# Retention values made in pass 1: one 256-column matmul for score and value, values kept in DRAM

## The chip, the cores and the metric

The kernel runs on one NeuronCore of a Trainium2 chip. A NeuronCore has a matrix engine (TensorE, PE in the profile), a vector engine (VectorE, DVE), a scalar engine (ScalarE, ACT), GpSimd (POOL) and SyncE (SP), which here only issues DMAs. Each engine works through its own list of instructions in order and waits on semaphores where an instruction needs another engine's result or a DMA. SBUF is the on-chip memory of 128 partitions, PSUM the accumulator memory that TensorE writes, in eight banks of 128 x 512 fp32. The metric is device time in microseconds (us), the median of several executions. All data is fp32.

## The reference, cut to what matters

The layer takes 64 sequences of 128 tokens of width 512. It adds a gated retention over a context, then a gated feed-forward network. `xn` is the layer-normed x; H is 4 heads of HD = 128.

```python
Q, K, V = (einsum('bshd,hde->bshe', heads(t), Wh) for t in (xn, ctx, ctx))
scores = einsum('bshe,bthe->bhst', Q, K) / sqrt(HD)
A = maximum(abs((scores * decay).sum(axis=0)), 1.0)      # summed over all 64 sequences
O = einsum('hst,bthe->bshe', A, V).reshape(b, s, dim)
Y = groupnorm(O) * gn_gamma + gn_beta
x = x + tanh(g_xattn) * ((relu(xn @ wg_w) * Y) @ wo_w)
x = x + tanh(g_ffn) * ffn(layernorm(x))                    # silu(gate) * up, then down
```

The sum over all sequences forces two passes: A needs the scores of every sequence before the first O can be made. Q and K share Wh, so the scores are xn (Wh Wh^T) ctx^T; the product Wh Wh^T is called `gram`.

## The kernel before, in words

The 64 sequences are worked in 16 groups of four (GB = 4, TOK = 512 tokens).

**Pass 1** loops over the groups. Iteration g runs three generators beside each other: `prepare` (L407: layer norm of group g, its transposition by TensorE into `xnT`), `scores` of group g-1 (L428) and `project` of group g-1 (L452: relu(xn wg) by seven products of a Strassen-like scheme, stored in DRAM as `w_scr` through ScalarE's DMA queue). `scores` makes, for each head, pq = gram x xnT over 512 columns (L432), copies it to SBUF by ScalarE (`q`, L436), and then adds for each of the 4 sequences and 4 heads a matmul of 128 columns into one PSUM bank (`acc`, L442), which gathers over all groups. The stationary operand of that matmul is the context tile c_t[j][:, h, :]. In the same iterations the weights of pass 2 are prepared (`prepare_weights`, L379): raw blocks are loaded by SP, summed by GpSimd and stored into `gu_scr`, `dn_scr` and `wo_scr`; two buffers hold raw blocks, so a block's load waits for an earlier block's store. SP's list also holds the loads of x (five tiles of two sequences, `load_x`, L103) and of context (five tiles of one sequence, `load_ctx`, L117).

Between the passes `acc` is multiplied by the decay, and its absolute value is clamped at 1 (L511 to L514): that is `attn`.

**Pass 2** runs the FFN of group g (`ffn`, L732) beside `attended` of group g+1 (L608: the wo products, the residual and the second layer norm) and `retention` of group g+2 (L527). `retention` loads the context a second time, makes the values V = ctx Wh by 16 matmuls of 128 columns (L534; stationary: the same c_t[j][:, h, :]), copies them to `v` by ScalarE (L538), multiplies by attn (`po`, L544), normalises and, through a DRAM round trip that transposes (`moved`, L187, with tiles of tag `sq` or `v`), scales w.

**The order of the work.** The generators are woven together by `interleave` (L30) in proportion to step counts written by hand. That gives a program order. The Tile framework then makes one list for each engine: it takes the instruction that is earliest in program order among those that its own estimate says are ready, so an instruction may move ahead of earlier ones, and loads go out as soon as a buffer of their tag is planned free. Buffers are given by tag: tiles of one tag share a fixed number of buffers (`bufs`), in program order. After the build the lists are fixed. `tc.issue_after` keeps weight traffic behind the last x load on SP.

PSUM holds three rotating banks under tag `mm` (ps_mm, L98) and five fixed ones (bank_a, bank_f, bank_b, bank_c0, bank_c1); `acc` is bank_c1 during pass 1.

Of the kernel before, what the change touches and what calls it, by code (L numbers as in the profile page):

```python
# [10 lines left out]
F32 = mybir.dt.float32  # L11
# [30 lines left out]
def after(steps, gen):  # L42

    for _ in range(steps):
        yield
    yield from gen
# [3 lines left out]
def flamingo_gated_layer(  # L50
# [36 lines left out]
    SQ = nc.vector.STREAM_SQUARE_SIZE  # L87
    NQ = P // SQ
# [2 lines left out]
    const = ctx.enter_context(tc.tile_pool(name="const", bufs=1))  # L91
    dram = ctx.enter_context(tc.tile_pool(name="dram", bufs=1, space=DRAM))
    xin = ctx.enter_context(tc.tile_pool(name="xin", bufs=5))
    cin = ctx.enter_context(tc.tile_pool(name="cin", bufs=5))
    att = ctx.enter_context(tc.tile_pool(name="att", bufs=1))
    wide = ctx.enter_context(tc.tile_pool(name="wide", bufs=2))
    stat = ctx.enter_context(tc.tile_pool(name="stat", bufs=4))
# [16 lines left out]
            pair.append(t)  # L114
        return pair

    def load_ctx(b):  # L117
        t = cin.tile([P, H, S], F32, tag="c", name="c_t")
        nc.sync.dma_start(out=t, in_=ctxT[b])
        return t  # L120

    x_next = [load_x(0, 1)]

# [4 lines left out]
    mean_var = const.tile([P, B, 2], F32, name="mean_var")  # L128
    rstd = const.tile([P, B], F32, name="rstd")
    attn = const.tile([P, H, S], F32, name="attn")  # L130
    wh_sb = const.tile([P, H, P], F32, name="wh_sb")
    gamma_sb = const.tile([P, NC], F32, name="gamma_sb")
    beta_sb = const.tile([P, NC], F32, name="beta_sb")
    gs_sb = const.tile([P, NI], F32, name="gs_sb")
# [10 lines left out]
        for n in range(2)  # L145
    ]
    w_scr = dram.tile([NG, 2, P, 2, TOK], F32, name="w_scr")

# [4 lines left out]
    bank_b = ps_bank.tile([P, TOK], F32, name="bank_b")  # L153
    bank_c0 = ps_bank.tile([P, TOK], F32, name="bank_c0")
    bank_c1 = ps_bank.tile([P, TOK], F32, name="bank_c1")
    for seeded in (bank_b, bank_c0):
        for i in range(TOK // P):
            nc.tensor.matmul(
                seeded[:, i * P : (i + 1) * P], lhsT=ident, rhs=ident,
                start=(i == 0), stop=True, skip_group_check=True,  # L160
            )
# [89 lines left out]


    pass1 = ExitStack()
    rows = pass1.enter_context(tc.tile_pool(name="rows", bufs=6))
    once = pass1.enter_context(tc.tile_pool(name="once", bufs=1))

    whT_sb = once.tile([P, H, P], F32, name="whT_sb")
# [7 lines left out]
                in_=wg[k * HN : (k + 1) * HN, e0 : e0 + P].rearrange("(k p) i -> p k i", p=P),  # L265
            )
    x_next.append(load_x(1))
    c_next = [load_ctx(b) for b in range(GB)]
# [4 lines left out]
    nc.scalar.activation(tanh_g, gates, AF.Tanh)  # L273


    gram = once.tile([P, H, P], F32, name="gram")
    pg = ps_mm.tile([P, H, P], F32, tag="mm", name="pg")
    for h in range(H):
        nc.tensor.matmul(
# [15 lines left out]
    def constants():  # L295

        nc.sync.dma_start(out=ds, in_=down_s.partition_broadcast(P))
        nc.sync.dma_start(out=decay, in_=decayT)
        nc.sync.dma_start(out=wh_sb, in_=wh.rearrange("h d e -> d h e"))
        nc.sync.dma_start(out=gamma_sb, in_=gamma.rearrange("(c p) -> p c", p=P))  # L300
        nc.sync.dma_start(out=beta_sb, in_=beta.rearrange("(c p) -> p c", p=P))
        nc.sync.dma_start(out=gs_sb, in_=gate_s)
        nc.sync.dma_start(out=us_sb, in_=up_s)

        cols = slice(REST * P, INTER)
        for m, mat, k in ((GA11, gateT, 0), (GA12, gateT, 1), (7, upT, 0), (GA22, upT, 1)):
            nc.sync.dma_start(
                out=gu_rest[:, m],
                in_=mat[k * HN : (k + 1) * HN, cols].rearrange("(c p) i -> p c i", p=P),
            )  # L310
# [91 lines left out]
            gu_rest[:, GA11], gu_rest[:, GA12], gu_rest[:, 7], gu_rest[:, GA22],  # L402
        )

    acc = bank_c1.rearrange("p (h s) -> p h s", h=H)

    def prepare(g, x_t, xnT):  # L407

        n = GB if g else 1
# [16 lines left out]
            yield  # L426

    def scores(g, c_t, xnT):  # L428
        qs = []
        for h in range(H):  # L430
            pq = ps_mm.tile([P, TOK], F32, tag="mm", name="pq")
            nc.tensor.matmul(  # L432
                pq, lhsT=gram[:, h, :], rhs=xnT[:, h, :], start=True, stop=True
            )
            q = rows.tile([P, TOK], F32, tag="row", name="q")
            nc.scalar.copy(q, pq)  # L436
            qs.append(q)
            if h % 2:
                yield
        for j in range(GB):  # L440
            for h in range(H):
                nc.tensor.matmul(  # L442
                    acc[:, h, :],
                    lhsT=c_t[j][:, h, :],
                    rhs=qs[h][:, j * S : (j + 1) * S],
                    start=(g == 0 and j == 0 and h == 0),
                    stop=(g == NG - 1 and j == GB - 1),
                    skip_group_check=True,
                )
            yield  # L450

    def project(g, xnT):  # L452

        b11, b12, b21, b22 = as_b(xnT)
        t = once.tile([P, 4, KC, HT], F32, tag="t1", name="t1")
        combine_b(nc.vector, [t[:, i] for i in range(4)], b11, b12, b21, b22)
        w = once.tile([P, 2, 2, TOK], F32, tag="w1", name="w1")
        m5 = once.tile([P, TOK], F32, tag="m5p", name="m5p")
# [24 lines left out]
        yield  # L483

    pending = None
    weights = prepare_weights()
    for g in range(NG):
        x_t, c_t = x_next.pop(0), c_next
        xnT = wide.tile([P, NC, TOK], F32, tag="xT", name="xnT")
        prep = prepare(g, x_t, xnT)  # L490
        next(prep)
        if g == 1:
            gate_weights()
            constants()
        elif g > 1:
            with tc.issue_after(last_load[0].ins):
                next(weights, None)
        interleave(
            (prep, GB),
            (scores(*pending) if pending else None, 2 + GB),  # L500
            (project(pending[0], pending[2]) if pending else None, 7),
        )
        x_next.append(load_x((g + 2) % NG))
        c_next = [load_ctx((g + 1) % NG * GB + j) for j in range(GB)]
        pending = (g, c_t, xnT)
    for _ in weights:
        pass
    interleave((scores(*pending), 1))


    nc.vector.tensor_mul(attn, acc, decay)  # L511
    absd = rows.tile([P, H, S], F32, tag="row", name="absd")
    nc.scalar.activation(absd, attn, AF.Abs)
    nc.vector.tensor_scalar_max(attn, absd, 1.0)  # L514

# [8 lines left out]
            ws.append(w)  # L524
        return ws

    def retention(g, c_t, ws):  # L527

        helper = nc.vector if g < 3 else nc.gpsimd
        v = att.tile([P, H, GB, P], F32, tag="v", name="v")  # L530
        for j in range(GB):
            pv = ps_mm.tile([P, H, P], F32, tag="mm", name="pv")
            for h in range(H):
                nc.tensor.matmul(  # L534
                    pv[:, h, :], lhsT=c_t[j][:, h, :], rhs=wh_sb[:, h, :],
                    start=True, stop=True,
                )
            nc.scalar.copy(v[:, :, j, :], pv)  # L538
            yield

        o = att.tile([P, GB, H, P], F32, tag="yT", name="o")
        for h in range(H):
# [7 lines left out]
                nc.scalar.copy(o[:, :, h, :], po)  # L550
            yield
        if g:
            sq = att.tile([P, NQ, NC, GB, SQ], F32, tag="v", name="sq")
        ons = []
        for j in range(GB):
            oj = o[:, j].rearrange("p h e -> p (h e)")
# [51 lines left out]
    def attended(g, x_t, ws, x1nT):  # L608
# [53 lines left out]
        yield  # L662

        if g:
            sq = att.tile([P, NQ, NC, GB, SQ], F32, tag="v", name="sq")
        for j in range(GB):
            xb = x_t[j // 2][:, j % 2, :]
            mv = stat.tile([P, 2], F32, tag="mv", name="mv")
# [14 lines left out]
            moved(x1nT, sq, sq_scr[1][g % 2])  # L683

    WAIT = 5
    RET_STEPS = 8 + WAIT + 2
    ATT_STEPS = 8 + GB

    def new_x1nT():
        return wide.tile([P, NQ, NC, GB, SQ], F32, tag="xT", name="x1nT")  # L690

    x_t, c_t = x_next.pop(0), c_next
    c_next = [load_ctx(GB + j) for j in range(GB)]
    ws = load_gate(0)
    interleave(
        (retention(0, c_t, ws), 12), (after(6, project(pending[0], pending[2])), 16),
    )
    x1nT = new_x1nT()
    pass1.close()
# [216 lines left out]

    def next_retention(g):

        nonlocal c_next, ws
        c_t = c_next  # L920
        ws = load_gate(g)
        yield from retention(g, c_t, ws)
        if g + 1 < NG:
            c_next = [load_ctx((g + 1) * GB + j) for j in range(GB)]

    def late_attended(g, x_t, x1nT):
        yield from attended(g, x_t, ws, x1nT)


    second = next_retention(1)  # L930
    interleave((attended(0, x_t, ws, x1nT), ATT_STEPS), (islice(second, 7), 10))
    pending = (0, x_t, x1nT, combine_tokens(nc.vector, x1nT))
    for g in range(NG - 1):
        x_t = x_next.pop(0)
# [4 lines left out]
        n_steps = ATT_STEPS + RET_STEPS  # L939
        if g == 0:  # L940
            steps.append(late_attended(1, x_t, x1nT))
            n_steps += RET_STEPS - 7
        if g + 2 < NG:
            steps.append(next_retention(g + 2))
        interleave(
# [62 lines left out]
```

## Time and profile before

| | |
|---|---|
| median of 3 runs | 2289.34 us (2286.19 to 2290.49) |
| the profiled execution | 2293.72 us |
| its span on the core | 2291.9 us |
| granted TensorE clock, mean | 0.999 of full |
| DMA traffic | 459.17 MB, mean 200 GB/s |
| HBM read / written | 376.72 MB / 80.61 MB |

The span is the time from the first to the last profiled instruction of the program. Busy time of an engine is the time in which it had an instruction at work; matmuls are pipelined, so the duration of one is longer than the distance to the next. Each fp32 matmul shows as two MATMUL records with a weight load (LDWEIGHTS, PEld) each. In lists of waits, "A <- B" says that A was released by B. SPq, ACTq are the issuing of DMAs.

### The profile page before, as it was taken

What the parts mean: (1) busy time and instruction counts of PE and PEld (TensorE: products, weight loads), DVE (VectorE), ACT (ScalarE), POOL (GpSimd) and SP (SyncE); (2) the same over time, 40 slices, a digit from 0 to 9 for tenths busy, and PEclk for the clock granted to TensorE, in tenths of its full rate; (3) what the DMA queues carried; (4) which work ended last, traced back from release to release, by engine and by line L of the source; (5) the groups of instructions that cost most, each with busy time, mean ns of one, the idle gap of its engine ahead of it and who ended that gap; (6) DMA issues with size and microseconds to landing.
All of it is one profiled execution on the core that took longest, in us unless ns stands there. A gap on an engine that the chain in (4) does not pass through costs nothing. (4 is left out here: it accounts for less than half of the span.)

```text
span 2291.9 us, 28061 instructions
## 1 busy us (share of the span) xinstructions
PE 2263.7 (99%) x10808; PEld 1945.1 (85%) x10808; DVE 861.6 (38%) x1771; ACT 574.7 (25%) x1052; POOL 674.5 (29%) x811
## 2 busy tenths in 40 slices
PE   8999999999999999999999999999999999999999
PEld 7777787888888888888888888888888888888888
DVE  6444534544333333323333423343433333333222
ACT  2333333312222221213131212121222122222221
POOL 4232202322232323232424232423223242323210
PEclk9999999999999999999999999999999999999999
DMA  8777746566565656665666656565657475645541
GB/s 266 264 232 244 248 161 228 189 195 225 178 226 173 219 187 212 197 220 193 218 197 197 208 191 225 181 214 181 214 171 236 158 236 174 230 155 186 167 149 65
DMA packets 158213, 459.17 MB, mean 200 GB/s; under 512 B 16768, under 2 KB 36864, under 8 KB 143360
## 3 DMA queue, kind: packets, MB, share of 16 engines
q1 hardware_dynamic: 152656, 440.34, 58.9%
q10 hardware_dynamic: 5424, 17.04, 1.8%
q8 instruction: 85, 1.39, 0.3%
q14 instruction: 48, 0.39, 0.1%
HBM read 376.72 MB, written 80.61 MB: 200 GB/s over the span
## 5 line engine op out<-in xcount | busy, mean ns | idle before, releaser
L207 PE MATMUL bank_c<-tcomb,gu 128*128 128x256 f32 x1920 | 456.9, 379 | 1.0 <-ACT bank_b L766 0.7
L207 PEld LDWEIGHTS bank_c<-tcomb,gu 128*128 128x128 f32 x1920 | 361.3, 190 | 49.4 <-ACT bank_b L766 1.5
L207 PE MATMUL bank_a<-x1nT,gu 128*128 128x256 f32 x1280 | 302.8, 379 | 1.1 <-ACT x1nT L677 0.7
L207 PEld LDWEIGHTS bank_a<-x1nT,gu 128*128 128x128 f32 x1280 | 242.1, 190 | 34.5 <-ACT x1nT L677 1.2
L247 POOL TENSOR_TENSOR hs<-h,h 128x256 f32<-128x256 f32 x80 | 58.0, 726 | 582.7 <-DVE h L746 582.7
L167 POOL TENSOR_TENSOR rs<-ve,mhalf 128x1 f32<-128x1 f32 x128 | 72.6, 576 | 486.4 <-DVE ve L166 471.2
L745 ACT ACTIVATE sil<-c,gs_sb 128x256 f32<-128x256 f32 x160 | 81.2, 508 | 322.7 <-DVE c L775 183.2
L603 POOL TENSOR_TENSOR w_t<-w_t,yT 128x256 f32<-128x256 f32 x112 | 77.9, 726 | 264.2 <-ACT yT L594 264.2
L207 PE MATMUL bank_b<-x1nT,gu 128*128 128x256 f32 x640 | 151.7, 379 | 0.0
L207 PE MATMUL bank_f<-tcomb,gu 128*128 128x256 f32 x640 | 151.2, 379 | 0.0
L798 PE MATMUL bank_c<-dn_w,hs 128*128 128x256 f32 x640 | 145.0, 382 | 0.0
L775 DVE TENSOR_TENSOR c<-bank_c,m 128x512 f32<-128x512 f32 x80 | 55.0, 688 | 237.6 <-PE bank_c L207 234.2
L798 PE MATMUL bank_f<-dn_w,h 128*128 128x256 f32 x640 | 143.4, 379 | 0.0
L798 PEld LDWEIGHTS bank_f<-dn_w,h 128*128 128x128 f32 x640 | 121.5, 190 | 22.4 <-issue 6.7
L207 PEld LDWEIGHTS bank_b<-x1nT,gu 128*128 128x128 f32 x640 | 121.6, 190 | 22.1 <-issue 6.2
L798 PEld LDWEIGHTS bank_c<-dn_w,hs 128*128 128x128 f32 x640 | 120.3, 190 | 19.7 <-ACT bank_b L875 4.0
L207 PEld LDWEIGHTS bank_f<-tcomb,gu 128*128 128x128 f32 x640 | 121.6, 190 | 16.6
L746 DVE SCALAR_TENSOR_TENSOR h<-bank_a,us_sb,sil 128x256 f32<-128x256 f32 x80 | 38.6, 482 | 240.2 <-ACT sil L745 240.2
L171 DVE BATCH_NORM_STATS2 st<-x_t 128x6 f32<-128x512 f32 x128 | 83.0, 684 | 103.3 <-DMA x_t<-in_x_dram 102.2
L758 ACT COPY bank_c<-bank_a 128x512 f32<-128x512 f32 x80 | 45.6, 570 | 258.6 <-PE bank_a L207 256.8
L746 DVE SCALAR_TENSOR_TENSOR h<-c,us_sb,sil 128x256 f32<-128x256 f32 x160 | 78.3, 489 | 75.1 <-ACT sil L745 75.1
L207 PE MATMUL bank_c<-t,wgc 128*128 128x256 f32 x384 | 92.5, 383 | 0.0
(166 smaller groups left out, 3518.1 us busy)
## 6 DMA issues: line engine op xcount, KB each, us to landing
gu<-gu_scr SPq DMA_DIRECT2D x80, 1024.0 KB, 4.9
dn_w<-dn_scr SPq DMA_DIRECT2D x112, 640.0 KB, 5.1
gu<-gu_scr SPq DMA_DIRECT2D x80, 768.0 KB, 5.9
c_t<-in_ctxT_dram SPq DMA_DIRECT2D x128, 256.0 KB, 4.3
x_t<-in_x_dram SPq DMA_DIRECT2D x62, 512.0 KB, 4.6
sq_scr<-sq SPq DMA_DIRECT2D x30, 1024.0 KB, 4.8
wo_w<-wo_scr SPq DMA_DIRECT2D x112, 256.0 KB, 3.9
w_scr<-w ACTq DMA_DIRECT2D x32, 512.0 KB, 5.8
```

Source lines behind the costliest of these rows:

```text
L167: nc.gpsimd.tensor_tensor(dst, ve, mhalf[:, :n], ALU.pow)
L171: nc.vector.bn_stats(st, src)
L207: nc.tensor.matmul(out, lhsT=w[:, s, k, :], rhs=x_k, start=(start and s == 0 and k == 0), stop=(s == 1 and k == KC - 1), skip_group_check= ...
L247: engine.tensor_tensor(s[0], a21, a22, ALU.add)
L603: (helper if d else nc.gpsimd).tensor_tensor(w, w, yT[:, :, d * KC + k, q * 2 : q * 2 + 2, :], ALU.mult)
L745: nc.scalar.activation(sil, src[:, 0:n], AF.Silu, scale=gs_sb[:, i : i + 1])
L746: nc.vector.scalar_tensor_tensor(dst, src[:, n : 2 * n], us_sb[:, i : i + 1], sil, ALU.mult, ALU.mult)
L758: nc.scalar.copy(bank_c, bank_a)
L775: nc.vector.tensor_add(c22, bank_c, m5)
L798: nc.tensor.matmul(bank[:, i * HN : (i + 1) * HN], lhsT=lhs[:, j, i * P : (i + 1) * P], rhs=dn[:, j, :], start=(start and i == 0 and j == ...
```

## The change

Values move from pass 2 to pass 1. `scores` no longer multiplies the context tile by q alone, but by two blocks of 128 columns at once: q of the sequence and Wh (both lie in one tile `qw`, whose last block holds Wh). The result, 256 columns, is the score part and the value part. Two sequences share one PSUM bank of tag `mm`: their score parts add up in its first block, their values stand in the second and third. One ScalarE copy takes the three blocks (128 x 384) to SBUF (`both`). The values are stored from there to a new DRAM tensor `v_scr`, two stores per group on SP's queue; the score parts are added by VectorE from SBUF into `attn`. The loop over heads is now outside that over sequences. `both` takes the tags `v`, `sq`, `ys` and `yT`, two of them per group in turn.

In pass 2 `retention` makes no values: `load_values` reads them with one load per group. The context isn't loaded a second time. The context pool has eight buffers instead of five and ends with pass 1. `sq` has a tag of its own, and `gram`, `m5p` and `absd` use tags of other tiles. Step counts of the weaving follow.

```diff
-    def load_ctx(b):
-        t = cin.tile([P, H, S], F32, tag="c", name="c_t")
-        nc.sync.dma_start(out=t, in_=ctxT[b])
-        return t
+    def load_ctx(g):
+        tiles = []
+        for j in range(GB):
+            t = cin.tile([P, H, S], F32, tag="c", name="c_t")
+            nc.sync.dma_start(out=t, in_=ctxT[g * GB + j])
+            tiles.append(t)
+        return tiles
...
-    for seeded in (bank_b, bank_c0):
+    for seeded in (bank_b, bank_c0, bank_c1):
...
-    rows = pass1.enter_context(tc.tile_pool(name="rows", bufs=6))
+    cin = pass1.enter_context(tc.tile_pool(name="cin", bufs=8))
...
+    qw = once.tile([P, H, GB + 1, P], F32, name="qw")
+    nc.sync.dma_start(out=qw[:, :, GB, :], in_=wh.rearrange("h d e -> d h e"))
...
-            q = rows.tile([P, TOK], F32, tag="row", name="q")
-            nc.scalar.copy(q, pq)
-            qs.append(q)
+            nc.scalar.copy(qw[:, h, 0:GB, :], pq)
             if h % 2:
                 yield
-        for j in range(GB):
-            for h in range(H):
-                nc.tensor.matmul(
-                    acc[:, h, :],
-                    lhsT=c_t[j][:, h, :],
-                    rhs=qs[h][:, j * S : (j + 1) * S],
-                    start=(g == 0 and j == 0 and h == 0),
-                    stop=(g == NG - 1 and j == GB - 1),
-                    skip_group_check=True,
-                )
+        for h in range(H):
+            if h % 2 == 0:
+                tags = ("v", "sq") if g % 2 else ("ys", "yT")
+                both = att.tile([P, 2, 2, 3, P], F32, tag=tags[h // 2], name="both")
+            for q in range(2):
+
+                sv = ps_mm.tile([P, 4, P], F32, tag="mm", name="sv")
+                for i in range(2):
+                    j = 2 * q + i
+                    nc.tensor.matmul(
+                        sv[:, 0 : 2 + i : 1 + i, :],
+                        lhsT=c_t[j][:, h, :],
+                        rhs=qw[:, h, j : GB + 1 : GB - j, :],
+                        start=(i == 0),
+                        stop=(i == 1),
+                        skip_group_check=True,
+                    )
+                nc.scalar.copy(both[:, h % 2, q], sv[:, 0:3, :])
+            if h % 2:
+                nc.sync.dma_start(out=v_scr[g, :, h - 1 : h + 1], in_=both[:, :, :, 1:3, :])
+                total = attn[:, h - 1 : h + 1, :]
+                for q in range(2):
+                    if g == 0 and q == 0:
+                        nc.vector.tensor_copy(total, both[:, :, 0, 0, :])
+                    else:
+                        nc.vector.tensor_add(total, total, both[:, :, q, 0, :])
             yield
...
-            (scores(*pending) if pending else None, 2 + GB),
+            (scores(*pending) if pending else None, 2 + H),
...
-        c_next = [load_ctx((g + 1) % NG * GB + j) for j in range(GB)]
+        if g + 1 < NG:
+            c_next = load_ctx(g + 1)
...
-    nc.vector.tensor_mul(attn, acc, decay)
-    absd = rows.tile([P, H, S], F32, tag="row", name="absd")
+    nc.vector.tensor_mul(attn, attn, decay)
+    absd = att.tile([P, H, S], F32, tag="m1", name="absd")
...
-    def retention(g, c_t, ws):
+    def load_values(g):
+        v = att.tile([P, H, GB, P], F32, tag="v", name="v")
+        nc.sync.dma_start(out=v, in_=v_scr[g].rearrange("p h q i e -> p h (q i) e"))
+        return v
+
+    def retention(g, v, ws):
 
         helper = nc.vector if g < 3 else nc.gpsimd
-        v = att.tile([P, H, GB, P], F32, tag="v", name="v")
-        for j in range(GB):
-            pv = ps_mm.tile([P, H, P], F32, tag="mm", name="pv")
-            for h in range(H):
-                nc.tensor.matmul(
-                    pv[:, h, :], lhsT=c_t[j][:, h, :], rhs=wh_sb[:, h, :],
-                    start=True, stop=True,
-                )
-            nc.scalar.copy(v[:, :, j, :], pv)
-            yield
...
-            sq = att.tile([P, NQ, NC, GB, SQ], F32, tag="v", name="sq")
+            sq = att.tile([P, NQ, NC, GB, SQ], F32, tag="sq", name="sq")
...
-    RET_STEPS = 8 + WAIT + 2
+    RET_STEPS = 4 + WAIT + 2
...
-        c_t = c_next
+        v = load_values(g)
         ws = load_gate(g)
-        yield from retention(g, c_t, ws)
-        if g + 1 < NG:
-            c_next = [load_ctx((g + 1) * GB + j) for j in range(GB)]
+        yield from retention(g, v, ws)
```

More of the change, by code (lines that the diff above doesn't have):

```diff
@@ L93, in flamingo_gated_layer @@
     xin = ctx.enter_context(tc.tile_pool(name="xin", bufs=5))
-    cin = ctx.enter_context(tc.tile_pool(name="cin", bufs=5))
     att = ctx.enter_context(tc.tile_pool(name="att", bufs=1))
@@ L130, in flamingo_gated_layer @@
     attn = const.tile([P, H, S], F32, name="attn")
-    wh_sb = const.tile([P, H, P], F32, name="wh_sb")
     gamma_sb = const.tile([P, NC], F32, name="gamma_sb")
@@ L147, in flamingo_gated_layer @@
     w_scr = dram.tile([NG, 2, P, 2, TOK], F32, name="w_scr")
+    v_scr = dram.tile([NG, P, H, 2, 2, P], F32, name="v_scr")
     bank_a = ps_bank.tile([P, TOK], F32, name="bank_a")
@@ L267, in flamingo_gated_layer @@
     x_next.append(load_x(1))
-    c_next = [load_ctx(b) for b in range(GB)]
+    c_next = load_ctx(0)
+    qw = once.tile([P, H, GB + 1, P], F32, name="qw")
+    nc.sync.dma_start(out=qw[:, :, GB, :], in_=wh.rearrange("h d e -> d h e"))
     gates = const.tile([P, 2], F32, name="gates")
@@ L273, in flamingo_gated_layer @@
     nc.scalar.activation(tanh_g, gates, AF.Tanh)
-    gram = once.tile([P, H, P], F32, name="gram")
+    gram = att.tile([P, H, P], F32, tag="wo", name="gram", bufs=3)
     pg = ps_mm.tile([P, H, P], F32, tag="mm", name="pg")
@@ L298, in constants @@
         nc.sync.dma_start(out=decay, in_=decayT)
-        nc.sync.dma_start(out=wh_sb, in_=wh.rearrange("h d e -> d h e"))
         nc.sync.dma_start(out=gamma_sb, in_=gamma.rearrange("(c p) -> p c", p=P))
@@ L403, in rest_weights @@
         )
-    acc = bank_c1.rearrange("p (h s) -> p h s", h=H)
     def prepare(g, x_t, xnT):
@@ L428, in scores @@
     def scores(g, c_t, xnT):
-        qs = []
         for h in range(H):
-            pq = ps_mm.tile([P, TOK], F32, tag="mm", name="pq")
+            pq = ps_mm.tile([P, GB, S], F32, tag="mm", name="pq")
             nc.tensor.matmul(
@@ L457, in project @@
         w = once.tile([P, 2, 2, TOK], F32, tag="w1", name="w1")
-        m5 = once.tile([P, TOK], F32, tag="m5p", name="m5p")
+        m5 = att.tile([P, TOK], F32, tag="m1", name="m5p")
         bank_c = bank_c0
@@ L664, in attended @@
         if g:
-            sq = att.tile([P, NQ, NC, GB, SQ], F32, tag="v", name="sq")
+            sq = att.tile([P, NQ, NC, GB, SQ], F32, tag="sq", name="sq")
         for j in range(GB):
@@ L690, in new_x1nT @@
         return wide.tile([P, NQ, NC, GB, SQ], F32, tag="xT", name="x1nT")
-    x_t, c_t = x_next.pop(0), c_next
-    c_next = [load_ctx(GB + j) for j in range(GB)]
+    x_t = x_next.pop(0)
+    v = load_values(0)
     ws = load_gate(0)
     interleave(
-        (retention(0, c_t, ws), 12), (after(6, project(pending[0], pending[2])), 16),
+        (after(3, retention(0, v, ws)), 11), (project(pending[0], pending[2]), 9),
     )
@@ L917, in next_retention @@
     def next_retention(g):
-        nonlocal c_next, ws
-        c_t = c_next
+        nonlocal ws
+        v = load_values(g)
         ws = load_gate(g)
-        yield from retention(g, c_t, ws)
-        if g + 1 < NG:
-            c_next = [load_ctx((g + 1) * GB + j) for j in range(GB)]
+        yield from retention(g, v, ws)
     def late_attended(g, x_t, x1nT):
@@ L930, in flamingo_gated_layer @@
     second = next_retention(1)
-    interleave((attended(0, x_t, ws, x1nT), ATT_STEPS), (islice(second, 7), 10))
+    interleave((attended(0, x_t, ws, x1nT), ATT_STEPS), (islice(second, 4), 8))
     pending = (0, x_t, x1nT, combine_tokens(nc.vector, x1nT))
@@ L941, in flamingo_gated_layer @@
             steps.append(late_attended(1, x_t, x1nT))
-            n_steps += RET_STEPS - 7
+            n_steps += RET_STEPS - 4
         if g + 2 < NG:
```

## The prediction

> **What bounds the kernel now.** First the busy table, then the same by stage (columns: stretch, its length, busy time of PE, PE weight load, DVE, ACT, POOL, each with its count; clock; DMA share; GB/s).
>
> ```profile
> PE 2263.7 (99%) x10808; PEld 1945.1 (85%) x10808; DVE 861.6 (38%) x1771; ACT 574.7 (25%) x1052; POOL 674.5 (29%) x811
> ...
> 20.00:340.00 320.00, 310.58 (x1660) 256.45 (x1659) 148.70 (x306) 107.25 (x178) 80.36 (x74) 1.00 0.70 234
> 340.00:396.00 56.00, 51.98 (x268) 40.67 (x267) 27.18 (x51) 20.66 (x36) 11.03 (x11) 1.00 0.59 212
> 396.00:2292.00 1896.00, 1889.33 (x8834) 1638.66 (x8832) 674.13 (x1387) 443.04 (x834) 574.41 (x711) 1.00 0.59 194
> ```
>
> TensorE is the bound in all stages, at full clock. Its idle time is 9.4 us in pass 1 (20 to 340), 4.0 in the passage to pass 2 (340 to 396), 6.7 in the long rest and 8 before 20 us. So a matmul saved is time saved, and a new wait of PE is time lost. The timeline shows what a matmul costs and where pass 1 waits (columns: start, duration, engine, line, tiles, count, and in brackets the idle time before it).
>
> ```profile
> 113.89 1.92 SPq L367 DMA_DIRECT2D gu_raw<-in_gateT_dram  x4
> ...
> 118.44 0.41 SPq L110 DMA_DIRECT2D x_t<-in_x_dram  x1
> 118.95 2.91 SPq L119 DMA_DIRECT2D c_t<-in_ctxT_dram  x3
> ...
> 120.45 1.06 PE L442 MATMUL bank_c<-q,c_t 128*128 128x128 f32 x8
> 121.34 1.89 PE L207 MATMUL bank_c<-t,wgc 128*128 128x256 f32 x8
> ...
> 123.07 1.89 PE L207 MATMUL bank_a<-xnT,wgc 128*128 128x256 f32 x8
> ...
> 124.50 1.29 DVE L171 BATCH_NORM_STATS2 st<-x_t 128x6 f32<-128x512 f32 x2 [6.14 <-DMA x_t<-in_x_dram]
> ...
> 126.49 0.68 DVE L423 COPY xnT<-pt 128x512 f32<-128x512 f32 x1
> ...
> 127.32 1.96 PE L432 MATMUL pq<-xnT,gram 128*128 128x512 f32 x4 [2.36 <-DVE xnT L423]
> ```
>
> Each fp32 matmul is two records (x512 at L442 for 256 matmuls). The durations overlap (pipelined); the cost is from start to start: eight records of 128 columns take 121.34 - 120.45 = 0.89 us, 0.111 each (0.112 over all L442 and L534 records); eight of 256 take 1.73, 0.216 each. The wait: SP loads the next raw weights only when the last sums have been stored; the x load stands behind them on SP; VectorE sits at the statistics of that x, and behind them is the xnT copy that PE needs. The waits (total, times, longest) of 20 to 350 us:
>
> ```profile
> PE pq L432 <- DVE xnT L423: 9.4, 5, 3.5
> SPq L119 <- PE bank_c L442: 115.2, 43, 11.2
> SPq L367 <- DMA gu_scr<-gu_raw: 40.4, 5, 10.6
> ```
>
> Five gate/up weight blocks, five stores waited for, five PE stalls, 1.9 us each. The stores are slow because the stretch after an iteration's start is full of traffic, while its end is not:
>
> ```profile
> 94.00:103.00 9.00, 9.00 (x57) 8.17 (x56) 4.33 (x10) 1.78 (x3) 4.97 (x6) 1.00 0.53 170
> 103.00:114.00 11.00, 11.00 (x52) 8.32 (x51) 5.65 (x12) 5.17 (x9) 1.23 (x1) 1.00 0.83 310
> ```
>
> **The change, part by part.**
>
> 1. PE passes. Removed: 256 score and 256 value matmuls of 128 columns, 1024 records x 0.112 = 114.7 us. Added: 256 of 256 columns, 512 records x 0.216 = 110.6. Net **-4.1 us**. Strided moving operands of 256 columns (x1nT at L207) already run at 0.216, so the two-block operand is taken at that; from below, -4.1 is all there is. A rule speaks against more: the Trainium skill, "TensorE: Matmul & The Clock Gate", section "Wait — 56ns, not 53.3ns?", says that a warm matmul costs its columns plus about 2.5 ns; by it, halving the count saves 512 x 2.5 = 1.3 us. The row's 8 ns per pair is used; the two differ by 2.8 us of 2292. The weight loads of 190 ns were never the bound: they ran at the 0.111 beat.
>
> 2. Where PE's work lies. A group of pass 1 gains 16 x 2 x (0.216 - 0.112) = 3.33 us of PE; a group of pass 2 loses 3.6.
>
> 3. ScalarE. Removed: 64 value copies of 581 ns, 37.2 us. Added: 128 copies of 128x384. Copies of 128x256 take 357 ns and of 128x512 570, so about 463, 59 us in pass 1, on an engine busy 107 of 320 us. Hidden by PE: two copies (0.93 us) per 1.73 us of matmuls, and the three PSUM buffers of `mm` let PE run two tiles ahead. If that cover fails (a copy queued behind the L477 relu, which waits for VectorE 77.0 us in 15 times) PE waits for a buffer; I put this at 0, and at up to 1.2 us in each of 15 iterations, 18 us, at the far end.
>
> 4. VectorE sums: four per group of 128x256 from SBUF, at 419 ns (row L603): 27 us, engine busy 149 of 320. No PE instruction waits for them before the end of pass 1; the prep work queued behind them on VectorE waits with them. Cost 0; covered by PE's 24 us per iteration.
>
> 5. DMA. Pass 1 gains 32 stores of 512 KB (16.8 MB) on SP; each waits for ScalarE copies, and behind it on SP stand raw weights, x and context loads. Gone from SP are most of the 115.2 us of waits for a context buffer: with eight there is room for a whole next group. But the heads are now the outer loop, so the four context tiles come free together, at the end of the scores, and four loads go out in a bunch at the iteration's end. Ahead of the late x load I therefore count both v stores and the three c_t loads that used to follow it (118.95 above): 2 x 0.524 + 3 x 0.262 = 1.83 MB. At the 310 GB/s of the full stretch that is 5.9 us. About 2.6 us of idle stretch (170 of 310 GB/s) before the boundary takes 1.2 us of it: x is 4.7 us later. PE has 3.33 us more to do before it runs dry, so each of the five stalls goes from 1.9 to 1.9 + 4.7 - 3.33 = 3.3 us: **+6.9 us**. Bounds: 0 lateness removes the stalls (-9.4), 5.9 gives +12.9. The skill's "DMA: Bandwidth & Descriptors", section "Specifications", puts the HBM limit of a core at about 358 GB/s; by it the lateness is 5.1 - 1.2 = 3.9, and the sum would be 4 us lower (2291). The row decides, as these are stores and loads mixed in this very stretch.
>
> 6. The passage. Its filler shrinks: the value matmuls of groups 0 and 1 (64 records each) were 7.1 us of PE work beside a chain of latencies (scores, attn, po, o statistics, transposes, w, wo products). Part 1 counts all of it as saved. v of group 0 must now be stored, landed and loaded: the last group's own sums use tag v, so its store (512 KB rows of pass 1: about 5 us) and then 1 MB (gu, 4.9 us) come first: with its first head pair done some 2.5 us before the last score matmul, -2.5 + 5 + 4.9, about 7.5 us after it, against 4.5 for the first po now (350.1 to 354.6). The gate projection of the last group, 12.1 us, covers that, but is then missing where PE already idles before L574 (1.4 us). I take **+3.0** of the 7.1 as not saved, ends 0 and 7.
>
> 7. Pass 2. One 1 MB load per group in place of four of 256 KB; equal bytes. Buffer v has one copy, but since sq has its own tag it is free from the end of one group's po to the next, about 115 us. SP issues loads as soon as a buffer is free (it waits for pv 28 times at L119), so its 4.9 us are hidden by the FFN's matmuls: 0. If the load went out only at its group's own start, 15 x 4.9 = 73 us; w_t, issued up to 320 us ahead in this trace, speaks against it.
>
> 8. wh's earlier load (0.9 us of DMA) and eight more seeding records lie in the start, before the first scores and while PE waits for whT (5.0 us): 0.
>
> Sum: -4.1 + 6.9 + 3.0 = **+5.8 us**. The profiled execution took 2293.7 (span 2291.9 and 1.8 around it), the median shown is 2289.3; the sum is laid on the median: **2295**. On the profile's own scale, a span of about 2298. A measurement can tell about 0.2% (4.6 us) from no change.
>
> **Rivals.**
>
> A. *Stalls vanish* (the other side, faster). One mechanism: the five stalls of L432, 1.9 us each. They are gone as soon as x comes less than 3.33 - 1.9 = 1.4 us later than now: SP no longer sits 115 us on context buffers, and PE has 3.33 us more cover. Then -4.1 - 9.4 + 3.0 = -10.5: 2279. Against it: 1.83 MB at 310 GB/s.
>
> B. *Nothing to see.* x comes about 3.3 us later, as late as the added cover; stalls stay 9.4. -4.1 + 3.0 = -1.1: 2288.
>
> C. *ScalarE becomes the gate of pass 1.* sv tiles need twice the PSUM turns (16 per group for 8), behind ScalarE's in-order waits for L476 and w_scr. With the 1.2 us of part 3: 2295 + 18 = 2313. For it: ACT idled 77.0 us at L477. Against: in the present pass no PE wait on ScalarE is in the list.
>
> **How the numbers follow.** Forecast 0.43 (2290 to 2303 by the bounds of parts 5 and 6), A 0.27, B 0.20, C 0.10. Of the forecast's own range a fifth lies within 0.2%, as does most of B and a little of A: faster 0.29, same 0.24, slower 0.47. Range 2278 to 2310: it takes in A's value and most of the way to C, leaving out one in ten on each side.
>
> **What would show it.** Right: 512 records of 256 columns at sv 0.216 apart; the five pq waits at 2 to 5 us; gu_scr stores landing later than 10.2 us; no L119 waits on scores; pv gone, L544 preceded by no long wait for v in pass 2. Wrong: pq waits gone (A); many PE waits for ScalarE's `both` copies (C); po waiting for v_scr loads group after group (part 7, tens of us); idle in 340 to 396 grown by more than 7.

## The result and the profile after

| | before | after |
|---|---|---|
| median | 2289.2 us (2286.19 to 2293.91) | 2293.05 us (2290.55 to 2294.8) |
| profiled execution, span | 2293.72, 2291.9 us | 2291.79, 2290.0 us |

The ratio of the times is 1.0015, 95% interval 1.0008 to 1.0022: slower by 3.9 us, which is less than the 0.2% that the prediction took as the limit of what can be told. The profiled pair shows the opposite, -1.9 us, because the profiled execution of before lay 4.5 us above its own median and that of after 1.3 below: -1.9 + 4.5 + 1.3 = 3.9. A trace of one execution tells here where time went between stages, but not the sign of the sum.

The page of the changed kernel, its busy table:

```profile
PE 2263.9 (99%) x10304; PEld 1925.2 (84%) x10304; DVE 901.7 (39%) x1835; ACT 601.5 (26%) x1116; POOL 670.9 (29%) x811
```

TensorE has 504 records less (512 by the change, and the eight more of seeding) and the same busy time to 0.2 us: a product that is held up shows partly as a longer one, as will be seen. The same by stage (columns: stretch, length, busy time of PE, PE weight load, DVE, ACT, POOL with counts; clock; DMA share; GB/s). The three stretches are again pass 1, the passage and the rest, but only roughly: the first ends 3.7 us behind the last score matmul here, and 10 us ahead of it in the table of before.

```profile
20.00:396.00 376.00, 375.56 (x1731) 306.21 (x1731) 185.61 (x381) 172.91 (x315) 79.11 (x74) 1.00 0.73 246
396.00:437.00 41.00, 34.44 (x143) 24.05 (x141) 24.81 (x51) 10.75 (x20) 11.68 (x12) 1.00 0.64 237
437.00:2290.00 1853.00, 1842.66 (x8377) 1584.87 (x8376) 680.88 (x1379) 415.21 (x778) 571.79 (x710) 1.00 0.60 199
```

In pass 1 TensorE is idle for 0.4 of 376 us, where it was idle for 9.4 of 320. In the rest it is idle for 10.3 us, where it was 6.7, though there is 50 us less to do. So the changed kernel has won in the one stage and lost in the other. The list of TensorE's waits in pass 1 has one line left:

```profile
PE pt L180 <- DVE xn L201: 0.4, 1, 0.4
```

The five pq stalls are gone in this execution (other traces of the changed kernel show some again, below). In the rest of the run another wait is new (total, times, longest):

```profile
PE bank_c L209 <- DVE c L788: 3.0, 14, 0.2
```

In the kernel before, the same add made TensorE wait once (396 to 2292 us):

```profile
PE bank_c L207 <- DVE c L775: 0.3, 1, 0.3
```

To see where the time went, I cut both traces at the same three events: the first pq matmul, the last score matmul, and the first FFN matmul that reads x1nT. The matmul work moved between the stages is counted in records: 512 sv records of 0.216 us less 512 score records of 0.112 give +53.2 us for pass 1, and the value matmuls of 14 groups, 448 records of 0.112, give -50.2 for pass 2.

| stage | before | after | difference | matmuls alone | gained (-) or lost (+) beyond them |
|---|---|---|---|---|---|
| to the first pq | 17.38 | 19.81 | +2.4 | 0 | +2.4 |
| pass 1, to the last score | 332.61 | 372.45 | +39.8 | +53.2 | -13.4 |
| passage, to the first FFN matmul | 45.58 | 42.78 | -2.8 | -7.1 | +4.3 |
| pass 2, to the end | 1896.32 | 1854.95 | -41.4 | -50.2 | +8.8 |
| sum, us | 2291.9 | 2290.0 | -1.9 | -4.1 | +2.1 |

The forecast's last column was 0, +6.9, +3.0, 0. Two large errors of opposite sign met in a sum that is nearly right. The experiments go after these two.

### The profile page after: what moved, and what is told of

It reads as the page before. It is cut to its first block, busy times and chain, and to the rows that moved or that the text cites. A ratio compares the mean times of both kernels' runs of the same rounds, so it can differ in the third digit from the quotient of the medians.

```text
span 2290.0 us, 27221 instructions
## 1 busy us (share of the span) xinstructions
PE 2263.9 (99%) x10304; PEld 1925.2 (84%) x10304; DVE 901.7 (39%) x1835; ACT 601.5 (26%) x1116; POOL 670.9 (29%) x811
## 4 chain that ended last, share of the span: by engine, by line
PE 93%; DVE 3%; POOL 1%; issue 1%; DMA 1%; ACT 0%; SPq 0%; ACTq 0%; POOLq 0%; DVEq 0%
PE bank_c L209 20%; PE bank_a L209 13%; PE bank_c L811 9%; PE bank_f L209 7%; PE bank_f L811 6%; PE bank_b L209 6%; PE sv L450 5%; PE by L635 4%; PE bank_b L811 3%; PE bank_a L811 3%; PE bz L635 2%; PE po L557 2%; PE pq L435 2%; PE bx L635 2%; PE bank_c L825 2%; PE pt L180 1%
## 5 line engine op out<-in xcount | busy, mean ns | idle before, releaser
L788 DVE TENSOR_TENSOR c<-bank_c,m 128x512 f32<-128x512 f32 x80 | 54.7, 684 | 228.6 <-PE bank_c L209 225.2
L450 PE MATMUL sv<-qw,c_t 128*128 128x256 f32 x512 | 120.6, 379 | 0.0
L646 POOL TENSOR_TENSOR x_t<-x_t,m 128x512 f32<-128x512 f32 x48 | 62.7, 1334 | 164.2 <-ACT m L652 152.5
L758 ACT ACTIVATE sil<-bank_a,gs_sb 128x256 f32<-128x256 f32 x80 | 37.9, 474 | 277.1 <-PE bank_a L209 277.1
```

The source lines that it names most:

```text
L450: nc.tensor.matmul(sv[:, 0 : 2 + i : 1 + i, :], lhsT=c_t[j][:, h, :], rhs=qw[:, h, j : GB + 1 : GB - j, :], start=(i == 0), stop=(i == 1), ...
L646: engine.tensor_tensor(dst, dst, src.rearrange("p (b d) -> p b d", b=2), ALU.add)
L758: nc.scalar.activation(sil, src[:, 0:n], AF.Silu, scale=gs_sb[:, i : i + 1])
L788: nc.vector.tensor_add(c22, bank_c, m5)
```

## The experiments

Each time is compared with the kernel before run on the same chip beside it, because the median of that kernel differed by up to 5.3 us from one set of runs to another (last section).

### The two kernels again

Both without an edit; they give the scatter and a second pair of traces.

> The kernel before, unchanged, profiled once more. Theory: the five waits of PE for the xnT copy in pass 1 (9.4 us in the first profile, whose execution at 2293.7 us was among the slowest of its kernel) depend on how fast the weight stores land and differ between executions; an execution nearer the median of 2289 shows 4 to 7 us of them. Rival: they are fixed, 9 to 10 us again, and the spread of 8 us between executions lies elsewhere.

> The changed kernel, unchanged, beside the kernel before on one more chip. The kernel before took 2289.2 us on the first chip and 2294.5 on the second, the changed one with five buffers 2293.0 on the second. Theory: the changed kernel has no DMA-dependent waits in pass 1 and is steady at 2292 to 2294, while the one before moves with its stalls, 2289 to 2295; the ratio is between 0.998 and 1.002 and depends on the chip. Rival: the change costs a fixed 3 to 4 us wherever it runs, ratio 1.0015 again.

Before: 2290.74 us in its profiled execution, the five pq stalls 6.9 us, stages of 16.74, 331.21, 45.19 and 1895.80. After: 2293.64 us against 2293.31 for before on that chip, ratio 1.0001 (0.9993 to 1.0009); stages 21.02, 373.55, 42.32, 1854.95. Against this second trace of before, whose execution lies nearer the median of the first set, the sum of the table would be +1.1 us instead of -1.9, and the gain in pass 1 12.0 us instead of 13.4.

Pass 2 repeats to 0.5 us. Pass 1 seems to repeat to 1.4, but two later runs (factors 1.00 and 1.15, below) edit only pass 2 of the changed kernel, so that every engine's list in pass 1 is the same, and there pass 1 took 375.98 and 376.35 us, with some of the pq stalls back. The wait in the second of them, 25 to 345 us:

```profile
PE pq L435 <- DVE xnT L425: 3.0, 4, 1.3
```

So pass 1 of the changed kernel lies between 372.45 and 376.35 us, and what it gains beyond its matmuls is 8 to 13 us.

### Why the pq stalls went: context buffers

My first theory was that SP no longer sits on context buffers. The kernel before gets eight of them in pass 1:

```diff
-    cin = ctx.enter_context(tc.tile_pool(name="cin", bufs=5))
+    cin[0] = pass1.enter_context(tc.tile_pool(name="cin", bufs=8))
...
+    cin[0] = ctx.enter_context(tc.tile_pool(name="cin2", bufs=5))
     c_next = [load_ctx(GB + j) for j in range(GB)]
```

> The kernel before, with eight context buffers in pass 1 and nothing else of the change (the context pool of pass 2 is made after pass 1, so the second loads for group 1 start later). Theory 'cover': the PE stalls of pass 1 went because each iteration has 3.33 us more of matmuls; then they stay here, 4 to 10 us, and the time is within 3 us of before. Theory 'buffers': they went because SP no longer waits for context buffers; then they are under 2 us here and the kernel is 4 to 8 us faster.

The converse, five in the changed kernel:

```diff
-    cin = pass1.enter_context(tc.tile_pool(name="cin", bufs=8))
+    cin = pass1.enter_context(tc.tile_pool(name="cin", bufs=5))
```

> The changed kernel with five context buffers instead of eight. Cover: no PE stalls in pass 1 come back, the time stays within 2 us of the changed kernel, near 2293. Buffers: the stalls of 1 to 4 us in the five gate/up iterations return, 2298 or more.

Before with eight: 2293.69 us, ratio 0.9995 (0.9987 to 1.0003). Its waits of TensorE and of SP, 20 to 350 us:

```profile
PE pq L433 <- DVE xnT L424: 7.5, 5, 2.2
```

```profile
SPq L119 <- PE bank_c L443: 111.6, 43, 11.2
```

The stalls stay, and so does SP's sitting on score matmuls (it was 115.2): with more buffers the builder moved only some of the context loads forward in SP's list. Nor did the change itself end these waits of SP. In the changed kernel, 20 to 396 us:

```profile
SPq L120 <- PE sv L450: 68.4, 30, 5.5
```

After with five: 2292.97 us, ratio 0.9994 (0.9988 to 1.0001), two pq waits of 0.5 us together. The number of context buffers shows in neither time.

### Why the pq stalls went: cover

The other theory: the late x load is still late, and TensorE now has work enough to cover it. The kernel before is given more work: each pq matmul is done twice (the second overwrites the first). Nothing else is edited, but the builder then orders parts of SP's and VectorE's lists of pass 1 differently, so its new order is a rival to the work.

```diff
-            nc.tensor.matmul(
-                pq, lhsT=gram[:, h, :], rhs=xnT[:, h, :], start=True, stop=True
-            )
+            for _ in range(2):
+                nc.tensor.matmul(
+                    pq, lhsT=gram[:, h, :], rhs=xnT[:, h, :], start=True, stop=True
+                )
```

> The kernel before with every pq matmul done twice into the same tile: 64 more matmuls of 512 columns, 128 records of 0.429 us, 3.43 us more PE work in each iteration of pass 1 and nothing else. Cover: the stalls for the xnT copy vanish, so the time grows by less than the work, 54.9 less 4 to 10, so +45 to +51 us, near 2338. Buffers: the stalls stay and it grows by 54 to 56, near 2344.

128 more records of 512 columns at 0.429 us are 54.9 us of work. The time went up by 43.6 (2338.08 against 2294.51 us, ratio 1.0187, 1.0171 to 1.0202), pass 1 by 45.0 against the other trace of before from that chip. All waits of TensorE from 14 to 440 us, down to 1 us:

```profile
PE pq L433 <- DVE mean_var L172: 1.9, 1, 1.9
PE pt L575 <- DVE o L565: 1.4, 1, 1.4
```

No pq waits for xnT any more, while SP still waits on score matmuls in that pass (192.2 us at L119). Some 10 us of the added work cost nothing: that is the stalls, with the short gaps around them. Whether the work did it or the new order is read from the timelines, as means over the five iterations with a gate/up block, in us after the iteration's first pq (the last row is an iteration without a stall):

| | before | pq doubled | changed kernel |
|---|---|---|---|
| the x load goes out | 14.7 | 13.1 | 15.5 |
| the last copy to xnT ends | 22.8 | 22.3 | 23.4 |
| TensorE reaches the next first pq | 21.0 | 24.4 | 24.2 |

With pq doubled the x load goes out 1.6 us sooner, but xnT is ready only 0.5 us sooner, while TensorE comes to it 3.4 us later. Of the 1.9 us of an average stall the order could have removed 0.5, so the cover removes the stalls.

In the changed kernel TensorE comes to it 3.2 us later and xnT is ready 0.6 later. So its x load hasn't become 4.7 us later. The timelines show why not. First the end of an iteration and the start of the next in the changed kernel, then SP's list behind it:

```profile
112.70 1.79 SPq L120 DMA_DIRECT2D c_t<-in_ctxT_dram  x4
115.29 0.88 SPq L460 DMA_DIRECT2D v_scr<-both  x1
116.26 1.87 SPq L395 DMA_DIRECT2D gu_scr<-gu_raw  x2
117.26 1.88 PE L435 MATMUL pq<-xnT,gram 128*128 128x512 f32 x4
...
130.56 2.00 SPq L371 DMA_DIRECT2D gu_raw<-in_upT_dram  x4
132.66 0.41 SPq L109 DMA_DIRECT2D x_t<-in_x_dram  x1
133.17 0.42 SPq L460 DMA_DIRECT2D v_scr<-both  x1
136.88 0.34 SPq L120 DMA_DIRECT2D c_t<-in_ctxT_dram  x1
```

The x load goes out 132.66 - 117.26 = 15.4 us after the iteration's first pq; before it was 118.44 - 103.86 = 14.6. It is 0.8 us later (0.7 in the mean of the five), not 4.7. Of the loads and stores that I had put ahead of it, this iteration's first v store goes out behind it (133.17), and the context loads either 3.6 us ahead of the gu stores, in the empty stretch (112.70), or also behind it (136.88).

### What the v stores cost

Only group 0's values are stored, and every group reads those back, so 15 of 16 pairs of stores are left out.

```diff
-                nc.sync.dma_start(out=v_scr[g, :, h - 1 : h + 1], in_=both[:, :, :, 1:3, :])
+                if g == 0:
+                    nc.sync.dma_start(out=v_scr[g, :, h - 1 : h + 1], in_=both[:, :, :, 1:3, :])
...
-        nc.sync.dma_start(out=v, in_=v_scr[g].rearrange("p h q i e -> p h (q i) e"))
+        nc.sync.dma_start(out=v, in_=v_scr[0].rearrange("p h q i e -> p h (q i) e"))
```

> The changed kernel with the stores of the values left out for all groups but the first; every group of pass 2 loads the values of group 0. 15.7 MB less are written in pass 1. Theory: the 3.33 us of cover per iteration hide all of it; the gu_scr stores land earlier (1 MB in about 10 us instead of 11.7) and the time stays within 2 us. Rival: the stores cost their lateness, and the time falls by 4 us or more.

2291.12 us, ratio 0.9993 (0.9984 to 1.0001) to before: about 2 us under the medians of the changed kernel, which come from other chips. Pass 1 is 372.52, inside the 372.45 to 376.35 with the stores. The DMA issues (KB each, median us to landing) of the changed kernel and then of this one:

```profile
v_scr<-both SPq DMA_DIRECT2D x32, 512.0 KB, 6.5
...
gu_scr<-gu_raw SPq DMA_DIRECT2D x5, 1024.0 KB, 11.7
```

```profile
gu_scr<-gu_raw SPq DMA_DIRECT2D x5, 1024.0 KB, 10.7
```

Before it was 10.2, and 10.9 in the second trace of the changed kernel, with all its stores. So a delay of the weight stores by the value stores is not shown, and in pass 1 the value stores cost nothing that stands out from its 4 us of scatter. The passage is 41.50 us, where the four traces of the changed kernel have 42.1 to 42.8, and its wait for the values of group 0 (0.9 us at L557 in the changed kernel) is gone.

### Where pass 2 lost its gain

Pass 2 runs one group per period. By its matmuls alone the period is 119.33 us before and 115.75 after; in the traces (mean of the middle twelve) it is 119.49 and 116.59, so the loss beside the FFN is 0.16 before and 0.84 after. The new wait stands here (changed kernel, timeline, in brackets the idle time before an instruction):

```profile
603.45 1.16 DVE L201 TENSOR_SCALAR xn<-x_t,mv,rs 128x512 f32<-128x512 f32 x2 [0.53 <-POOL rs L169]
603.76 1.89 PE L209 MATMUL bank_b<-x1nT,gu 128*128 128x256 f32 x8
604.53 0.70 DVE L185 STREAM_TRANSPOSE sq<-xn 128x512 f32<-128x512 f32 x1
605.16 0.65 DVE L788 TENSOR_TENSOR c<-bank_c,m 128x512 f32<-128x512 f32 x1
605.87 1.99 PE L209 MATMUL bank_c<-tcomb,gu 128*128 128x256 f32 x8 [0.21 <-DVE c L788]
607.70 1.89 PE L209 MATMUL bank_f<-tcomb,gu 128*128 128x256 f32 x8
```

VectorE normalises and transposes a part of the other generators' work (L201, L185) before it makes the sum `c` (L788), and only that add frees bank_c for TensorE's next product. The list shows a wait of 0.21 us, but the product starts 605.87 - 603.76 = 2.11 us after the one before it in place of 1.73, and takes 1.83 to the next: 0.48 us lost, once per group. A second place, the product into bank_c at L825, behind a burst of `retention`, costs 0.22 per group by the same reckoning. Together 0.70, which with the 0.16 of before gives about the 0.84.

That is a matter of which step of `attended` or `retention` meets which step of the FFN, and the constant in `interleave` that shifts it is the 1.05 in the last line of pass 2. If so, the constant moves the loss, in either direction.

```diff
-            (ffn(*pending), FFN_STEPS), (chain(*steps), int(n_steps * 1.05)),
+            (ffn(*pending), FFN_STEPS), (chain(*steps), int(n_steps * 1.00)),
```

> The changed kernel with the weave of pass 2 at 1.00 of the step count instead of 1.05, so the attention work of a group is issued a little earlier against its FFN. Theory: the 0.8 us lost in each of 14 groups of pass 2 is an accident of where VectorE's norm and transposes fall beside the FFN's own adds; another weave moves the stalls: the loss per group changes to anything between 0 and 2 us, and the time by -11 to +15 us. Rival: it comes from the value matmuls missing as filler; then it stays at 0.7 to 0.9 us per group and the time within 2 us.

The same with 1.15:

> The same with 1.15: attention work issued later. Alignment: a loss per group different from 0.8 us, the time -11 to +15 us. Filler: 0.7 to 0.9 us per group again, within 2 us.

And the kernel before with 1.15, to see whether the constant is simply better for both:

> The kernel before with weave 1.15. It loses only 0.08 us per group of pass 2 (119.41 us per group against 119.33 of matmuls), so there is nothing to win: same within 2 us, or slower where the bursts fall badly (up to 1 us per group, 14 us).

| kernel | factor | period, us | time, us | ratio to before |
|---|---|---|---|---|
| after | 1.05 | 116.59 | 2293.64 | 1.0001 (0.9993 to 1.0009) |
| after | 1.00 | 116.44 | 2294.21 | 1.0002 (0.9994 to 1.0011) |
| after | 1.15 | 116.17 | 2289.03 | 0.998 (0.9973 to 0.9987) |
| before | 1.05 | 119.44 | 2293.09 | 1 |
| before | 1.15 | 120.76 | 2306.18 | 1.006 (1.0046 to 1.0074) |

With 1.00 the wait at L788 goes, and another comes in its place (first line: total, times, longest); with 1.15 the kernel before gets two new ones:

```profile
PE bank_c L825 <- DVE c L858: 3.6, 13, 0.3
```

```profile
PE bx L622 <- POOL w_t L603: 5.2, 13, 0.4
PE bank_c L812 <- DVE c L845: 3.5, 13, 0.5
```

(The times of after are from one chip, where before took 2293.31, those of before from another, and the period of before at 1.05 is that of its second trace; the ratio is what compares.) The same number helps the one kernel by some 4.6 us and costs the other 13.1. For before 1.05 was a good alignment; after the change, which took 4 steps and the value matmuls and copies from `retention`, it no longer was. Which of these shifted it the runs don't separate.

The rival is that the value matmuls were needed as filler, work that hides such waits. The run with 1.00 alone doesn't decide: its loss per group is 0.69 us and its time within 0.6 us, as the rival has it. But 1.15 leaves a loss of 0.42 and 1.25 (below) one of 0.17, as small as before, and neither has a value matmul in pass 2.

### The start

The changed kernel's first pq comes 2.4 us later than before in the first pair; over four traces of it the first pq lies at 19.8 to 21.1 us, over three of before at 16.7 to 17.5. Here is the start of before, then that of the changed kernel, in the timeline:

```profile
11.90 0.90 DVE L199 TENSOR_SCALAR xn<-x_t,mean_var,rstd 128x512 f32<-128x512 f32 x1
...
15.36 1.29 DVE L171 BATCH_NORM_STATS2 st<-x_t 128x6 f32<-128x512 f32 x2 [2.56 <-DMA x_t<-in_x_dram]
```

```profile
13.67 0.69 DVE L173 BATCH_NORM_STATS2 st<-x_t 128x6 f32<-128x512 f32 x1 [3.43 <-DMA x_t<-in_x_dram]
14.28 1.06 DVE L201 TENSOR_SCALAR xn<-x_t,mean_var,rstd 128x512 f32<-128x512 f32 x1
15.39 0.86 PE L180 MATMUL pt<-ident,xn 128*128 128x128 f32 x4 [3.99 <-DVE xn L201]
```

VectorE's statistics of the next x, which it waits for, stand ahead of the first group's xn, and TensorE waits 3.99 us for that. Before, they stood behind it. Two things that the change put into the start could have done this: the eight seeding records of bank_c1, with which the builder drew up VectorE's list in another order, or the earlier load of wh. This run moves the seeding behind the loop of pass 1 (`seed` is the old loop as a function; its last call stands there) and leaves the load:

```diff
-    for seeded in (bank_b, bank_c0, bank_c1):
...
+    seed(bank_b, bank_c0)
...
         pending = (g, c_t, xnT)
+    seed(bank_c1)
```

> The changed kernel with the third bank seeded after the loop of pass 1 instead of at the start (eight records of 128 columns, 0.9 us, warm). Theory: the eight more seeding records at the start shift the order made for VectorE, so that the statistics of the second x stand ahead of the first group's norm; without them the first pq is back from 19.8 to about 17.4 us and the time falls by 1 to 2 us. Rival: the earlier load of wh delays x(1); then the first pq stays at 19.8 and the time grows by about 1 us.

The first pq is at 16.13 us, VectorE's statistics of the next x (14.10) stand behind xn again, and wh's load goes out at 12.10 us, for 12.21: the seeding was the cause. The time is 2290.87, ratio 0.9988 (0.9981 to 0.9995), 2.8 us under the changed kernel on this chip. The start alone is 3.7 to 4.9 us shorter than in the two traces of the changed kernel; pass 1, at 375.11, lies within what it takes there.

### Both together

Late seeding with 1.15, and with 1.25:

> The changed kernel with both mends: late seed of the third bank and weave 1.15. Theory: the two losses lie in different stages and add: 4.6 and 2.8 us less than the changed kernel's 2293.6, about 2286.5, some 6 us or 0.3% under the kernel before. Rival: one chip's ordering hides the other, about 2289.

> The same with weave 1.25. If the position of VectorE's bursts is what matters, the loss per group differs again from 0.4 us (1.15): between 0 and 1.5 us, the time 2281 to 2302; if later is simply better, 2285 or less.

2285.87 us, ratio 0.9969 (0.9958 to 0.998), and 2281.86 us, ratio 0.9955 (0.9942 to 0.9969). The second beats both kernels. Its period is 115.92, 0.17 above its matmuls, as before; its pass 2 takes 1845.96, 50.4 less than before, where 50.2 of matmuls went. The same stretch of its timeline as above:

```profile
602.03 1.89 PE L212 MATMUL bank_b<-x1nT,gu 128*128 128x256 f32 x8
602.30 0.69 DVE L792 TENSOR_TENSOR c<-bank_c,m 128x512 f32<-128x512 f32 x1 [1.64 <-PE bank_c L212]
603.76 1.89 PE L212 MATMUL bank_c<-tcomb,gu 128*128 128x256 f32 x8
```

The add that makes `c` now starts 0.27 us after TensorE's product begins, VectorE having waited for the bank and not the bank for VectorE, and the next product follows at 1.73.

## Why the prediction was right or wrong

The time was right (2295 for 2293.05), and so was the direction, slower by less than can be told from no change. Three of the reasons were not, and that the sum came out is luck.

**Part 1 held.** 512 sv records, 0.216 us apart, with the moving operand in two separate blocks of 128 columns: by this beat -4.1 us, as forecast. In the timeline of the changed kernel the eight records of 104.29 us take 106.02 - 104.29 = 1.73:

```profile
104.29 1.89 PE L450 MATMUL sv<-qw,c_t 128*128 128x256 f32 x8
106.02 1.89 PE L209 MATMUL bank_c<-t,wgc 128*128 128x256 f32 x8
```

**Parts 3 and 4 held.** The groups' table of the changed kernel:

```profile
L458 ACT COPY both<-sv 128x384 f32<-128x384 f32 x128 | 61.1, 478 | 37.3 <-PE sv L450 35.8 <-DMA dn_scr<-dn_t 0.7
L466 DVE TENSOR_TENSOR attn<-attn,both 128x256 f32<-128x256 f32 x62 | 29.9, 482 | 46.8 <-ACT both L458 46.7
```

478 ns where 463 was forecast, and 482 for 419; the copies wait for TensorE and not TensorE for them. Rival C is out.

**Part 5 failed,** at the step "ahead of the late x load I therefore count both v stores and the three c_t loads". That gave L = 4.7 us; the trace has 0.8. The step took a load's place from the order in which its buffer comes free, and added each transfer to the same full stretch; in SP's list, part of them went out before the stretch and part behind x. The formula of that step was right: with 0.8, 1.9 + 0.8 - 3.33 is below nothing, and the stalls vanish, as they did in the first trace. With so little to spare, -0.6 us, an x load that is slower in one execution brings some back, as in the run with 1.15 (3.0 us in four). The doubled pq shows that the 3.33 us of part 2 do it, and not the order of the lists. Rival A's mechanism thus happened, by its second reason and not by its first: SP's waits for context buffers are ruled out by the two runs on buffers, and 68.4 of the 115.2 us of them stayed. In the profiled pair it gained 13.4 us (8 to 13 over all traces), 9.4 of it in the list of waits. The other 4 no line names; some 2.4 of them lie in the iterations without a stall, which grew by 3.17 us each (21.01 to 24.18) and not by 3.33.

**Part 6 was right in kind.** v of group 0 is loaded late and po waits for it (0.86 us), then the transposition waits for o (1.30):

```profile
392.67 0.33 SPq L547 DMA_DIRECT2D v<-v_scr  x1
398.67 1.10 PE L557 MATMUL po<-v,attn 128*128 128x512 f32 x2 [0.86 <-DMA v<-v_scr]
410.12 0.44 PE L587 MATMUL pt<-ident,o 128*128 128x128 f32 x2 [1.30 <-DVE o L577]
```

The first po came 398.67 - 392.26 = 6.4 us after the last score matmul, for 7.5 forecast and 4.5 before. Not saved were 4.3 us of the 7.1, for 3.0. (The 7.1 are the 64 records of both groups together, 32 each, not 64 each.) How the 4.3 divide between the late v and the missing filler stays open: a buffer of its own for v of group 0 wasn't tried. Without the stores that wait is gone and the passage 0.6 to 1.3 us shorter, so the late v accounts for about that much of it.

**Part 7 failed,** at "0". It looked for the cost of the v load, and rightly found none: no po of pass 2 waits for v in TensorE's list. The cost was elsewhere: 50.2 us of matmuls, and four steps, were taken out of a weave whose alignment they were part of, and 8.8 us were lost to VectorE's order beside the FFN. The factors of the weave show it: on the changed kernel the loss moves with them, down to that of before at 1.25, and before loses at 1.15.

**Part 8 failed,** at "0": +2.4 us in the first pair, by VectorE's order at the start; the late seeding shows it.

So the sum was -4.1 + 6.9 + 3.0 = +5.8 in the forecast and, in the profiled pair, -4.1 + 2.4 - 13.4 + 4.3 + 8.8 = -1.9 us (parts rounded). The medians say +3.9 in the first set of runs and +0.3 in the second. That the forecast met the first median is therefore the luck of errors that cancelled, and partly of the runs.

## What to carry to other kernels

Where the bounding engine stalls for a late transfer, count how much work the change puts in front of that stall: added work of the bound engine can be free up to the stall's length. When steps are taken out of an interleaved stage, its proportions were tuned with them in it, and have to be tuned again before the change is judged: here two small edits turned no gain into -0.45%. A transfer's place in a queue is read from the trace's issue times; it is not derived from when a buffer comes free.

## What the runs showed of the hardware

- A wait of TensorE of 0.21 us cost 0.48 us from start to start (above), so the list's 3.0 us over 14 waits stood for some 6.7. In this kernel, with TensorE 99% busy, the sum of listed waits was a lower bound.
- The kernel before, unchanged, had medians of 2289.2, 2294.5, 2293.3 and 2293.1 us in four sets of runs, the last three on three different chips; the changed kernel had 2293.05 and 2293.64. A difference of 0.2% between two kernels can only be read from runs made side by side, and even then it was 1.0015 in one set and 1.0001 in another.
- A moving operand of two blocks, up to 512 columns apart, costs TensorE the same 0.216 us per record as one block of 256.
